# A gated cross-attention block in FP32 on one core: outputs of the last four pairs summed two by two in one PSUM bank

## The chip, the cores and the metric

The kernel runs on one core of one Trainium2 chip. A core has five engines that run side by side, each with its own queue of instructions: PE (matrix multiply, TensorE), DVE (VectorE), ACT (ScalarE), POOL (GpSimd) and SP (SyncE, which here only issues DMAs). They wait for each other through semaphores. Matmuls read SBUF and write PSUM, which has eight banks of 128 x 512 FP32 values; DVE and ACT read PSUM[...].

The metric is the device time of one execution in microseconds (us). Lower is better. Times in the profile count from the start of its span.

## The reference

32 sequences of 64 tokens, width 512, 32 heads of 128. Attention over a context, then a gated feed-forward layer with LoRA:

```python
q = (layernorm(x) @ Wq); k = (ctx @ Wk); v = (ctx @ Wv)          # split into 32 heads
score = einsum("bqhd,bkhd->bhqk", q, k) / sqrt(128) + position_bias   # masked keys: -inf
probs = softmax(score)
x = x + tanh(g0) * (einsum("bhqk,bkhd->bqhd", probs, v) @ Wo)
x = x + tanh(g1) * (layernorm(x) @ weight.T + bias + LoRA(layernorm(x)))
```

## The kernel before

The 2048 tokens are worked in two halves (`p` = 0, 1) of 1024. In a half, 16 pairs of heads (`n` = 0 to 15) follow each other. The times of half one stand below without a mark; half two repeats the same program on the other tokens.

**Numbers in two parts.** A FP32 product is made of three matmuls in FP32R: each operand is split into a high part (a cast on ACT) and a low part (operand minus high part, a subtraction on POOL or DVE), and `mm3` (L92) adds high x high, high x low and low x high into one bank. Products of keys, queries and values are done by Strassen's scheme with seven block products p1, p6, p7, p5, p2, p4, p3 (`unit`, L348), each of six matmuls of 128 x 512; p4 and p3 of a unit are worked after the first product of the next unit (`carry`). The seven blocks of the activations, high and low, fill seven big tiles, one for each name.

**Stages of a half.** `stage_a` (L654) makes keys and values of all pairs and stores them in device memory. `attention` (L739) then goes pair by pair: `q_unit` makes the queries; `scores` multiplies them with the keys (L807), adds bias and mask, takes the row maximum on DVE (L811) and subtracts it on POOL (L812); `exped` takes the exponential on ACT (L821); `normed` sums rows on DVE (L831 to L833) and scales on POOL (L834); `turn` transposes 32 x 32 blocks on DVE (L845), and `copy` (L842) places 32 x 256 pieces in the block diagonal tile `pts`, on ACT, or straight from the scores by a DVE transpose. `pv` (L938) multiplies values and probabilities into four banks (L943) and evicts each as high part `ch` on ACT (L946) and low part `cl` on DVE (L947). `prep_o` (L960) splits the output weight of a pair (L89 on ACT, L90 on POOL) from a raw tile fetched earlier; `oproj` (L973) multiplies `ch` and `cl` of a pair with it, tile of 128 tokens by tile, six matmuls each (`pa`), and adds the bank to the running output `acc` on DVE (L981).

**Order.** The program is written in order by hand; there is no scheduler. What goes beside the products is kept in generators in the list `streams`: each call of `beat()` after a product advances every stream by one step, and `drain` runs a stream to its end. So the order in the queue of each engine is fixed by where a stream starts and how many beats pass.

**The end of a half.** After the scores of pairs 14 and 15 the loop (L1076) does: output product 12 for tiles 0 to 5, first half of values 13, tiles 6 and 7 of product 12, second half of values 13, and the same for 13 with 14 and 14 with 15; then product 15. Weight 13 begins to be split (`start_o`) after tiles 0 to 5 of product 12, weights 14 and 15 one product later each. `last_turned` (L893) is the stream that normalizes and turns pairs 14 and 15; its inner `rest` turns pair 15. In half one, `next_blocks` (L455) splits the context of half two into its seven blocks beside this, on POOL mostly (raw `c1`, blocks `c1p`), and all are done before `stage_a` of half two starts. In half two, `ffn_weights` (L1128) splits the weights of the feed-forward layer instead, and `beside` works its first chunk (`ffn_tile`: transposes `tpf`; `ffn_lora`: products `pt`) between the tiles of output product 14.

Of the kernel before, what the change touches and what calls it, by code (L numbers as in the profile page):

```python
# [43 lines left out]
def flamingo_block(ctx: ExitStack, tc: tile.TileContext, x, xT, ctxT, bias, mask, gx, gf,  # L44
# [410 lines left out]
    def next_blocks(f, tags, nm, out):  # L455
        b11, b21, b12, b22 = parts(f)

        def block(q, raw, eng=nc.gpsimd):
            t = big(tags[ORDER.index(q)], [P, 2, 2, 512], F32R, f"{nm}{q}")
            out[q] = []  # L460
            for kt in range(2):
                split(raw[kt], t[:, 0, kt], t[:, 1, kt], eng)
                out[q].append((t[:, 0, kt], t[:, 1, kt]))
                yield

        def sub(o, a, b, eng=nc.gpsimd):
            for kt in range(2):
                eng.tensor_tensor(o[kt], a[kt], b[kt], ALU.subtract)
                yield

        yield from block("p1", b11)
        yield from block("p3", b22)
        yield from sub(b11, b12, b11)
        yield from sub(b12, b22, b12)
        yield from sub(b22, b22, b11, nc.vector)
        yield from block("p6", b22)
        yield from block("p7", b12)
        yield from block("p5", b11)
        yield from block("p2", b21)
        yield from sub(b21, b21, b22, nc.vector)  # L480
        yield from block("p4", b21, nc.vector)
# [172 lines left out]
    def stage_a(p, first, fc, res, rot, more, enter):  # L654
        xc, plain = first
        f = None
        for n in range(NPR):
            g = p * NPR + n
            if n == 0 and plain:
                sums = sum_blocks(fc, res, f"c{p}", nc.vector, xc)  # L660
                streams.append(sums)
            if n == (1 if plain else 0):
                streams.append(key_blocks(p, n + 1))
# [75 lines left out]
    def attention(p, res, rest, freed):  # L739
# [6 lines left out]
        def load_v(n, t=None, cs=None):  # L746
            b["v", n] = t or big(res[3], [P, NT, 256], F32, f"v{p}_{n}")
            for sl in [slice(c * 4, c * 4 + 4) for c in cs] if cs else [slice(0, NT)]:
                nc.sync.dma_start(out=b["v", n][:, sl], in_=vd[p][n // 2][:, sl, n % 2 * 256:(n % 2 + 1) * 256])
# [50 lines left out]
        acc, pts = [], []  # L800

        def scores(n, i, qT, kT):
            ps = psum(f"ps{p}_{n}_{i}", (P, NT, S))
            for t in range(NT):
                for h in range(2):
                    tok = slice(t * P + h * S, t * P + (h + 1) * S)
                    nc.tensor.matmul(ps[h * S:(h + 1) * S, t, :], qT[:, i, tok], kT[:, i, tok], start=True, stop=True)  # L807
            s = sm[n % 2][:, i]
            nc.vector.scalar_tensor_tensor(s, ps, SCALE, s, ALU.mult, ALU.add)
            mx = st.tile([P, NT], F32, tag="mx", name=f"mx{p}_{n}_{i}")  # L810
            nc.vector.tensor_reduce(mx, s, AX.X, ALU.max)  # L811
            nc.gpsimd.tensor_tensor(s, s, mx.unsqueeze(2).to_broadcast([P, NT, S]), ALU.subtract)  # L812
            beat()
            if n:
                streams.append(exped(s))
            else:
                nc.scalar.activation(s, s, AF.Exp)
# [75 lines left out]
        def last_turned():  # L893
            n = NPR - 2
            pts.append(big(res[1], [P, 2, NT, P], F32, f"pz{p}"))
            tp, todo = {}, []
            norm = both(normed(n, 0), normed(n + 1, 0))

            def turn_next(m, i):
                if i == 0:  # L900
                    tp[m] = [rows.tile([P, NT, S], F32, tag="row", name=f"tp{p}_{m}_{k}") for k in range(2)]
                turn(tp[m][i], m, i)
                todo.extend((m, i, q) for q in quads)
# [4 lines left out]
            def copies(k):  # L908
                for m, i, q in todo[:k]:
                    copy(nc.scalar.copy, m, i, tp[m][i], *q)  # L910
                del todo[:k]

            for k in range(14):
                if k in (0, 1, 8, 10):
                    next(norm)
                if k in (3, 5):
                    turn_next(n, k // 5)
                if k in (4, 9):
                    zero(k // 9)
                copies(2 if k in (4, 5, 8, 9, 12, 13) else 1)  # L920
                yield
            copies(16)

            def rest():
                for i in range(2):
                    turn_next(n + 1, i)
                    yield
                while todo:
                    copies(2)
                    yield  # L930
            b["s", n + 1] = rest()
            streams.append(b["s", n + 1])

        def both(*gs):
            for g in gs:
                yield from g

        def pv(n, cs=(0, 1)):  # L938
            drain(b["s", n])
            for i, c in [(i, c) for i in range(2) for c in cs] if n == 0 else [(i, c) for c in cs for i in range(2)]:  # L940
# [5 lines left out]
                nc.scalar.copy(ch[:, i, sl], ps)  # L946
                nc.vector.tensor_tensor(cl[:, i, sl], ps, ch[:, i, sl].bitcast(F32), ALU.subtract)  # L947
                beat()
            if NPR - 3 <= n < NPR - 1:
                load_v(n + 1, b["v", n], cs)  # L950
            elif n + 1 < NPR:
# [8 lines left out]
        def prep_o(n):  # L960
            raw = raw_of.pop(("o", p * NPR + n))
            t = big(res[2 if n in (NPR - 3, NPR - 1) else 4], [P, 2, 1024], F32R, f"wo{p}_{n}")
# [10 lines left out]
        def oproj(n, ts=range(NT), beside=None):  # L973
            drain(ob.get(n))
            w = b["o", n]
            for t in ts:
                ps = psum(f"pa{p}_{n}_{t}")
                sl = slice(t * P, (t + 1) * P)
                mm3(ps, [((ch[:, i, sl], cl[:, i, sl]),
                          (w[:, 0, i * 512:(i + 1) * 512], w[:, 1, i * 512:(i + 1) * 512])) for i in range(2)])  # L980
                nc.vector.tensor_tensor(acc[t], ps, acc[t], ALU.add)  # L981
                if n == NPR - 1 and p < NPH - 1:
                    nc.sync.dma_start(out=x1d[t * P:(t + 1) * P, :], in_=acc[t])
                beat()
                if beside:
                    beside(t)
# [8 lines left out]
        def run(xq, prefetch, before_last, last_unit, last, beside=None):  # L995
# [28 lines left out]
            def score(*ns):  # L1024
# [11 lines left out]
                elif n == NPR - 2:  # L1036
                    b["s", n] = last_turned()
# [23 lines left out]
            for a in range(4, NPR, 2):  # L1061
# [5 lines left out]
                if a < NPR - 2:  # L1067
                    oproj(a - 2)
                    start_o(a - 1)
# [5 lines left out]
            for n in range(NPR - 3, NPR):  # L1075
                oproj(n - 1, range(6), beside if n == NPR - 1 else None)  # L1076
                if n == NPR - 3:
                    start_o(n)
                pv(n, (0,))
                oproj(n - 1, range(6, NT))  # L1080
                pv(n, (1,))
                if n < NPR - 1:
                    start_o(n + 1)
            drain(ob[n])
            last(lambda t: oproj(n, range(t, t + 1)), acc)
# [42 lines left out]
    def ffn_weights(tags):  # L1128
# [6 lines left out]
        for _ in range(6):  # L1135
# [12 lines left out]
        for t in range(4):  # L1148
            ffn_norm(0, t)
            yield  # L1150
# [50 lines left out]
    def ffn_chunk(c, beside=lambda t: None):  # L1201
        more = c + 1 < NPH * NCH
        if c:
            ffn_lora(c)
# [10 lines left out]
    more = None  # L1215
    for p in range(NPH):
# [8 lines left out]
        enter, run = attention(p, res, rest, freed)  # L1225
        xq = stage_a(p, first, f, res, rot, more, enter)
        if p < NPH - 1:
# [10 lines left out]
            def last_unit():  # L1238
                blocks = paced(next_blocks(f, qt, f"c{p + 1}", first[0]), 2)
                keys = prep("k", g, nc.gpsimd, 36, then=lambda: fetch("k", g + 2, "r0"))  # L1240
                streams.extend((blocks, keys))
                parts_of.extend((blocks, keys))

            def last(o, acc):
                nonlocal more
                for t in range(NT):
                    o(t)
                for d in parts_of:
                    drain(d)
                more = acc_stats(p, acc)  # L1250
            parts_of = []
            run(xq, prefetch, before_last, last_unit, last)
        else:
# [4 lines left out]


            def beside(t):  # L1260
                if t == 0:
                    drain(weights)
                if t < 4:
                    ffn_tile(0, t)
                elif t == 4:
                    ffn_lora(0)
                else:
                    ffn_norm(1, 0)

            def last(o, acc):  # L1270
                acc1.extend(acc)

                def moments(t):
                    ln_moments(acc[t], mv2[:, p * NT + t, :], f"r{p}_{t}")

                def rstd_of(c):
                    for _ in ln_rstd(mv2[:, c * 4:(c + 1) * 4, :], f"f{c}", rstd, c, 5, nc.gpsimd):
                        pass

                def rest_of(t):  # L1280
                    if t < 2:
                        moments(4 + 2 * t)
                        moments(5 + 2 * t)
                    if t == 1:
                        rstd_of(NPH * NCH - 1)
                    if t == 3:
                        ffn_norm(2, 0)

                for t in range(NT):
                    o(t)  # L1290
                    if t < 4:
                        moments(t)
                    if t == 3:
                        rstd_of(NPH * NCH - 2)
                ffn_chunk(0, rest_of)
                ffn_chunk(1, lambda t: ffn_norm(3, 0) if t == 3 else None)
                ffn_chunk(2)
                ffn_chunk(3)
            run(xq, ffn_fetch, ffn_rows, last_unit, last, beside)
# [45 lines left out]
```

## Time and profile before

| what | us |
|---|---|
| median of three runs | 1537.7 (1535.86 to 1538.94) |
| profiled execution | 1537.11 |
| its span, first to last instruction | 1535.3 |
| PE busy | 1522.2 (99%) |
| POOL busy | 1045.5 (68%) |
| DVE busy | 959.8 (63%) |
| ACT busy | 727.5 (47%) |
| mean DMA rate | 162 GB/s |

A line of groups in the profile gives: source line, engine, operation, output and input tiles, sizes and count, then busy time and mean nanoseconds of one, then the idle time of the engine just before them and what ended it. A line of waits gives: who waited for whom, total us, how often, longest. A line of the timeline gives: start, length, engine, line, operation, tiles, count, and in brackets the idle time before it and its releaser. The time of a matmul in a row is longer than its step, since matmuls overlap. A busy PE is no PE at full speed: at half clock it is busy too.

### The profile page before, as it was taken

How to read it: one execution, taken by the hardware profiler on the slowest of the kernel's cores; microseconds unless marked ns; L12 is line 12 of the kernel's file. 1: busy time of each engine (PE TensorE's matmuls, PEld its weight loads, DVE VectorE, ACT ScalarE, POOL GpSimd, SP SyncE). 2: the span in 40 equal slices, each digit the busy share in tenths (PEclk: the TensorE clock that was granted, in tenths of full speed). 3: DMA queues.
4: the chain of work that ended last, by engine and by line, in shares of the span. 5: the costliest groups of instructions: out<-in, count | busy, mean ns of one | idle time of the engine just before them, and what ended most of it. 6: DMA issues, size and time to landing. Idle time of an engine off the chain costs nothing.

```text
span 1535.3 us, 25153 instructions
## 1 busy us (share of the span) xinstructions
PE 1522.2 (99%) x8988; PEld 1282.3 (84%) x8988; DVE 959.8 (63%) x1599; ACT 727.5 (47%) x1602; POOL 1045.5 (68%) x1154
## 2 busy tenths in 40 slices
PE   9999999999999999999999999999999999999998
PEld 7888888888888888887888888888888888888787
DVE  5665554376676567667476558437657666766764
ACT  6444233355654565467344423335566456546611
POOL 3898478968665667577789847896866666656210
PEclk9999999999999999999999999999999999999999
DMA  6754544384244354522575454438425435442311
GB/s 216 264 192 151 199 165 167 138 309 172 102 150 167 107 210 138 179 83 83 200 253 202 154 201 168 168 140 315 158 89 170 147 132 185 151 166 78 96 42 69
DMA packets 111135, 248.51 MB, mean 162 GB/s; under 512 B 10305, under 2 KB 44097, under 8 KB 106914
## 3 DMA queue, kind: packets, MB, share of 16 engines
q1 hardware_dynamic: 110722, 246.38, 45.7%
q8 instruction: 71, 1.16, 0.3%
q10 hardware_dynamic: 288, 0.52, 0.1%
q14 instruction: 54, 0.44, 0.1%
HBM read 173.45 MB, written 73.42 MB: 161 GB/s over the span
## 4 chain that ended last, share of the span: by engine, by line
PE 96%; DVE 1%; POOL 1%; ACT 1%; issue 0%; DMA 0%; DVEq 0%; POOLq 0%; ACTq 0%
PE pa L98 23%; PE po L943 7%; PE pzv L98 6%; PE pvv L98 6%; PE pxv L98 6%; PE pxq L98 5%; PE pzq L98 5%; PE pvq L98 5%; PE pzk L98 5%; PE pvk L98 5%; PE pxk L98 5%; PE ps L807 4%; PE pyv L98 3%; PE pf L98 3%; PE pyq L98 3%; PE pyk L98 3%
## 5 line engine op out<-in xcount | busy, mean ns | idle before, releaser
L98 PE MATMUL pa<-wo,ch 128*128 128x512 f32 x1024 | 321.9, 395 | 6.3 <-POOL wo L90 3.4
L98 PEld LDWEIGHTS pa<-wo,ch 128*128 128x128 f32 x1024 | 191.1, 189 | 47.8 <-POOL wo L90 5.2
L842 ACT COPY pt<-tp 32x256 f32<-32x256 f32 x472 | 190.4, 403 | 68.1 <-DVE tp L845 57.1
L981 DVE TENSOR_TENSOR acc<-pa,acc 128x512 f32<-128x512 f32 x256 | 171.2, 679 | 57.0 <-PE pa L98 56.9
L98 PE MATMUL pa<-wo,cl 128*128 128x512 f32 x512 | 200.7, 392 | 0.0
L760 POOL TENSOR_TENSOR sm<-sm,madd 128x512 f32<-128x512 f32 x60 | 76.8, 1293 | 107.2 <-DMA sm<-bias 107.2
L947 DVE TENSOR_TENSOR cl<-po,ch 128x512 fp32r<-128x512 f32 x128 | 87.7, 691 | 58.7 <-ACT ch L946 58.2
L834 POOL TENSOR_TENSOR sm<-sm,r 128x512 f32<-128x512 f32 x64 | 67.0, 1046 | 76.6 <-DVE r L833 69.0
L943 PEld LDWEIGHTS po<-pt,v 128*128 128x128 f32 x960 | 112.5, 192 | 3.6 <-ACT pt L842 0.9
L98 PEld LDWEIGHTS pa<-wo,cl 128*128 128x128 f32 x512 | 96.7, 189 | 20.8 <-DVE cl L947 0.5
L943 PE MATMUL po<-pt,v 128*128 128x128 f32 x960 | 113.1, 275 | 0.6 <-DVE pt L842 0.6
L356 DVE TENSOR_TENSOR vt<-pvv,vt 128x512 f32<-128x512 f32 x64 | 44.1, 689 | 93.3 <-PE pvv L98 93.3
L90 POOL TENSOR_TENSOR wo<-rawo,wo 128x512 fp32r<-128x512 f32 x64 | 82.3, 1309 | 28.3 <-ACT wo L89 17.5
L946 ACT CAST ch<-po 128x512 fp32r<-128x512 f32 x128 | 75.0, 589 | 46.4 <-PE po L943 44.4
L812 POOL TENSOR_TENSOR sm<-sm,mx 128x512 f32<-128x512 f32 x64 | 67.0, 1051 | 43.0 <-DVE mx L811 43.0
L356 DVE TENSOR_TENSOR qT<-pvq,qT 128x512 f32<-128x512 f32 x64 | 44.1, 690 | 73.1 <-PE pvq L98 73.0
L356 DVE TENSOR_TENSOR kT<-pvk,kT 128x512 f32<-128x512 f32 x60 | 41.3, 688 | 76.2 <-PE pvk L98 76.2
L378 ACT COPY vt<-pxv 128x512 f32<-128x512 f32 x32 | 18.9, 589 | 130.9 <-PE pxv L98 130.9
L821 ACT ACTIVATE sm<-sm 128x512 f32<-128x512 f32 x60 | 38.0, 633 | 85.6 <-POOL sm L812 82.4
L356 DVE TENSOR_TENSOR qT<-pzq,qT 128x512 f32<-128x512 f32 x64 | 44.2, 691 | 37.8 <-PE pzq L98 37.6
L807 PEld LDWEIGHTS ps<-kB,qT 128*64 128x64 f32 x2048 | 61.3, 138 | 4.2 <-issue 2.1
L192 POOL TENSOR_TENSOR vs<-wvr,wvr 128x512 f32<-128x512 f32 x24 | 31.3, 1313 | 49.2 <-DMA wvr<-wv 49.2
(992 smaller groups left out, 3777.2 us busy)
## 6 DMA issues: line engine op xcount, KB each, us to landing
kd<-kT SPq DMA_DIRECT2D x64, 512.0 KB, 3.8
vd<-vt SPq DMA_DIRECT2D x128, 256.0 KB, 2.4
kB<-kd SPq DMA_DIRECT2D x32, 1024.0 KB, 10.0
v<-vd SPq DMA_DIRECT2D x28, 1024.0 KB, 7.9
rawq<-wq SPq DMA_DIRECT2D x32, 512.0 KB, 3.3
sm<-bias SPq DMA_DIRECT2D x64, 256.0 KB, 5.0
rawo<-wo SPq DMA_DIRECT2D x32, 512.0 KB, 3.6
rawk<-wk SPq DMA_DIRECT2D x31, 512.0 KB, 5.3
```

The source lines that it names most:

```text
L90: eng.tensor_tensor(lo, raw, hi.bitcast(F32), ALU.subtract)
L98: nc.tensor.matmul(ps, a, b, start=start and i == 0, stop=stop and i == 3 * n - 1, skip_group_check=True)
L356: nc.vector.tensor_tensor(o, ps, i, ALU.add)
L760: nc.gpsimd.tensor_tensor(t, t, masks[p][0], ALU.add)
L807: nc.tensor.matmul(ps[h * S:(h + 1) * S, t, :], qT[:, i, tok], kT[:, i, tok], start=True, stop=True)
L812: nc.gpsimd.tensor_tensor(s, s, mx.unsqueeze(2).to_broadcast([P, NT, S]), ALU.subtract)
L834: nc.gpsimd.tensor_tensor(t, t, r.unsqueeze(2).to_broadcast([P, NT, S]), ALU.mult)
L842: f(pts[n == NPR - 2][dst, i, :, src], of[src, :, ki * 32:(ki + 1) * 32])
L943: nc.tensor.matmul(ps[:, t * P:(t + 1) * P], b["v", n][:, c * 4 + t, i * P:(i + 1) * P], pts[n == NPR - 2][:, i, c * 4 + t, :], start=True ...
L946: nc.scalar.copy(ch[:, i, sl], ps)
L947: nc.vector.tensor_tensor(cl[:, i, sl], ps, ch[:, i, sl].bitcast(F32), ALU.subtract)
L981: nc.vector.tensor_tensor(acc[t], ps, acc[t], ALU.add)
```

## The change

The end of each half is worked in another order.

- Pairs 12 and 13, and 14 and 15, share their output products: `oproj2` adds both pairs' matmuls (12 for each tile) in one bank, and DVE adds it to `acc` once.
- All values of 13 are multiplied right after the last scores, before any output product of 12. Values 14 and 15 are multiplied half by half between the two joint products' parts: first halves after tiles 0 to 5 of 12+13, second halves after tiles 6 and 7.
- `ch` and `cl` of pairs 13 and 15 lie in two other big tiles (`more_ctx`, the places of activation blocks p2 and p4); weight 13 lies in p5's place, weights 14 and 15 in the two tiles of the queries.
- Weight 13 begins to be split before the last scores, weight 14 after values 13, weight 15 after the first part of the joint product.
- `last_turned` turns both pairs in 16 steps; pair 15's second head goes by direct DVE transposes.
- Three of the seven context blocks of half two wait for these tiles: p5 until all values are read, p2 and p4 until the half has ended. p2 and p4 are then split on DVE within the first key unit of half two.
- The row maxima have four small buffers instead of two.
- In half two the norms, moments and transposes of chunk 0 go beside the last joint product, and its LoRA product stands in `ffn_chunk` behind them.

```diff
-    def next_blocks(f, tags, nm, out):
+    def next_blocks(f, tags, nm, out, gate):
...
         yield from block("p7", b12)
+        while not gate:
+            yield
         yield from block("p5", b11)
-        yield from block("p2", b21)
+        while len(gate) < 2:
+            yield
+        yield from block("p2", b21, nc.vector)
         yield from sub(b21, b21, b22, nc.vector)
         yield from block("p4", b21, nc.vector)
...
+            if n == 1 and not plain:
+                drain(blocks)
...
-            mx = st.tile([P, NT], F32, tag="mx", name=f"mx{p}_{n}_{i}")
+            mx = st.tile([P, NT], F32, tag="mx", name=f"mx{p}_{n}_{i}", bufs=4)
...
+            direct = [(n + 1, 1, q) for q in quads]
...
+            for k in range(16):
+                if k in (1, 3, 6, 8):
                     next(norm)
+                if k in (4, 5):
+                    turn_next(n, k - 4)
+                if k in (5, 7):
+                    zero(k // 7)
+                if k == 9:
+                    turn_next(n + 1, 0)
+                if k > 5:
+                    for of, m, i, q in todo[:3]:
+                        copy(nc.scalar.copy, m, i, of, *q)
+                    del todo[:3]
+                if k > 10:
+                    for m, i, q in direct[:2]:
+                        copy(nc.vector.transpose, m, i, sm[m % 2][:, i], *q)
+                    del direct[:2]
+                yield
...
-            t = big(res[2 if n in (NPR - 3, NPR - 1) else 4], [P, 2, 1024], F32R, f"wo{p}_{n}")
+            if n < NPR - 2:
+                t = big(qt[3] if n == NPR - 3 else res[4], [P, 2, 1024], F32R, f"wo{p}_{n}")
+            else:
+                t = kqp.tile([P, 2, 1024], F32R, tag="kq", name=f"wo{p}_{n}")
...
+        def oproj2(n, ts, lead, beside=None):
+            drain(ob[n])
+            ts = list(ts)
+            for group in [ts[:lead]] + [[t] for t in ts[lead:]]:
+                ps = [psum(f"pa{p}_{n}_{t}") for t in group]
+                for k, t in enumerate(group):
+                    mm3(ps[k], o_terms(n, t), stop=False)
+                    beat()
+                drain(ob[n + 1])
+                for k, t in enumerate(group):
+                    mm3(ps[k], o_terms(n + 1, t), start=False)
+                    nc.vector.tensor_tensor(acc[t], ps[k], acc[t], ALU.add)
...
+                    beat()
+                    if beside:
+                        beside(t)
...
-                    start_o(a - 1)
+                start_o(a - 1)
+                if a < NPR - 2:
                     pv(a - 1)
                 score(a, a + 1)
...
-            for n in range(NPR - 3, NPR):
-                oproj(n - 1, range(6), beside if n == NPR - 1 else None)
-                if n == NPR - 3:
-                    start_o(n)
-                pv(n, (0,))
-                oproj(n - 1, range(6, NT))
-                pv(n, (1,))
-                if n < NPR - 1:
-                    start_o(n + 1)
-            drain(ob[n])
-            last(lambda t: oproj(n, range(t, t + 1)), acc)
+            n = NPR - 4
+            load_v(n + 3)
+            pv(n + 1)
+            start_o(n + 2)
+            oproj2(n, range(6), 3)
+            start_o(n + 3)
+            for c in range(2):
+                if c:
+                    oproj2(n, range(6, NT), 1)
+                pv(n + 2, (c,))
+                pv(n + 3, (c,))
+            values_read(acc)
+            oproj2(n + 2, range(NT), 2, beside)
...
-        for _ in range(6):
+        for _ in range(8):
             yield
...
-        if c:
-            ffn_lora(c)
+        ffn_lora(c)
...
             def beside(t):
-                if t == 0:
-                    drain(weights)
                 if t < 4:
-                    ffn_tile(0, t)
-                elif t == 4:
-                    ffn_lora(0)
+                    ffn_norm(0, t)
+                    moments(t)
                 else:
-                    ffn_norm(1, 0)
+                    ffn_tile(0, t - 4)
+                if t == 4:
+                    rstd_of(NPH * NCH - 2)
```

## The prediction

> **What bounds the kernel now.** I read the page first. Its line of PE says 99% busy and its chain of waits puts 96% on PE, so only time in which PE stands or runs slowly can be won or lost. The waits of PE say where it stands:
>
> ```profile
> PE   9999999999999999999999999999999999999998
> PE pa L98 <- POOL wo L90: 3.4, 4, 1.0
> PE pa L98 <- ACT wo L89: 2.8, 2, 1.7
> ```
>
> Both are output products (pa) waiting for a split output weight. The timeline puts them at the end of each half, where pair 13's weight comes too late:
>
> ```profile
> 693.09 0.62 ACT L89 CAST wo<-rawo 128x512 fp32r<-128x512 f32 x1
> 693.76 0.50 PE L98 MATMUL pa<-wo,ch 128*128 128x512 f32 x1 [1.67 <-ACT wo L89]
> 695.12 0.50 PE L98 MATMUL pa<-wo,ch 128*128 128x512 f32 x1 [0.85 <-POOL wo L90]
> ```
>
> The windows of that stage give the length, then busy PE, and third from the end the granted clock:
>
> ```profile
> 1418.60:1421.50 2.90, 0.73 (x4) 0.22 (x2) 1.39 (x3) 2.82 (x7) 2.53 (x3) 0.94 0.00 0
> 1421.50:1428.00 6.50, 5.47 (x12) 3.92 (x13) 6.15 (x11) 5.01 (x12) 3.66 (x3) 0.50 0.41 127
> 690.00:697.00 7.00, 3.91 (x23) 2.83 (x22) 5.90 (x11) 6.79 (x16) 5.84 (x6) 1.00 0.08 28
> ```
>
> A matmul of 512 columns starts every 0.227 us (six take 1.36 in the timeline). Gaps over that step in the PE rows are 3.7 us at 691.8 to 696.5, and 6.4 us at 1418.5 to 1428, of which 3.0 us are some fifteen matmuls at half clock: 10.1 us in all. Check: 192 output matmuls (43.6) and three value products (3.5 each) make 54.1 us of work after half one's last score; PE took from 677.33 to 735.74, 58.4.
>
> What the new order asks for hangs on the softmax of pairs 14 and 15, which starts here in the two halves:
>
> ```profile
> 676.72 2.54 POOL L760 TENSOR_TENSOR sm<-sm,madd 128x512 f32<-128x512 f32 x2 [10.58 <-DMA sm<-bias]
> 1403.56 2.54 POOL L760 TENSOR_TENSOR sm<-sm,madd 128x512 f32<-128x512 f32 x2 [9.38 <-DMA sm<-bias]
> ```
>
> POOL had idled 10 us for pair 15's bias. The durations I use:
>
> ```profile
> L812 POOL TENSOR_TENSOR sm<-sm,mx 128x512 f32<-128x512 f32 x64 | 67.0, 1051 | 43.0 <-DVE mx L811 43.0
> L834 POOL TENSOR_TENSOR sm<-sm,r 128x512 f32<-128x512 f32 x64 | 67.0, 1046 | 76.6 <-DVE r L833 69.0 <-ACT pt L842 5.5 <-DMA sm<-bias 1.2
> L90 POOL TENSOR_TENSOR wo<-rawo,wo 128x512 fp32r<-128x512 f32 x64 | 82.3, 1309 | 28.3 <-ACT wo L89 17.5 <-PE tpf L137 10.8
> L947 DVE TENSOR_TENSOR cl<-po,ch 128x512 fp32r<-128x512 f32 x128 | 87.7, 691 | 58.7 <-ACT ch L946 58.2
> L468 DVE TENSOR_TENSOR c<-c,c 128x512 f32<-128x512 f32 x4 | 5.4, 1352 | 0.8 <-POOL c1p L90 0.8
> L842 DVE STREAM_TRANSPOSE pt<-sm 32x256 f32<-32x256 f32 x8 | 3.4, 423 | 0.1
> ACT sm L821 <- POOL sm L812: 82.4, 59, 5.6
> ```
>
> [...]
>
> **The change part by part.**
> *Nothing on PE goes.* The matmuls of the tail are the same. 32 of the 64 adds into acc in the two tails go, 32 x 0.68 = 22 us of DVE, beside matmuls: worth 0.
>
> *Weight 13 early* (start_o before the last scores): the 10.1 us go, half clock included. But its two POOL subtractions (2 x 1.31) now stand among the maxima subtractions of pairs 14 and 15.
>
> *Values 13 ahead of the output products, all evicted before product 12+13.* Half one, POOL without a break from 676.72 in the new order: mask twice 2.54, L812 of 14, context block p1 1.31, weight 13 1.31, L812, weight 13, L812 of 15: 2.54 + 3 x 1.05 + 3 x 1.31 = 9.6, to 686.3. ACT has exp of 15 first half (0.63), then the first eviction of values 13 (0.59): 687.6. Next in ACT is block p3's cast and the second exp of 15, for which POOL does p1's other half and L812 (2.4, to 688.7); exp to 689.35, the second eviction to 689.95, its low part on DVE (0.69) to 690.65. PE: values 13 from 677.33 to 680.8, 18 matmuls of pair 12 (4.1) to 684.9. The first tile's six matmuls of pair 13 would end at 686.3; their last needs the low part of 690.65 and ends at 690.9. **Lost 4.6.** The evictions stand behind the exponentials[...].
>
> *Values 14 and 15 both before tiles 6 and 7 of product 12+13.* Before, 15's came 25 us later. POOL goes on after DVE's row sum of 14 (1.1, to 691.75): two L834 of 14, p3 1.31, two context differences 1.27, weight 14 2 x 1.31, L834 of 15, a difference 1.29, L834 of 15: 12.0 with 0.2 of waiting, to 703.9. DVE then makes 15's second head by eight direct transposes (8 x 0.42), with two L468 (2.7) and an add (0.68) between: 6.8, to 710.7. PE: 690.9 + 2 x 1.36 + 3 x 2.72 = 701.8, values 14 first half 1.75, values 15 would end at 705.3. It ends at 711.6. **Lost 6.3.** The copies of 15's first head on ACT (tp at 702.8, 8 x 0.40) end at 706, inside this.
>
> *Half two*, with no context blocks but the FFN weights: POOL 1403.56 + 2.54 + 3 x 1.05 + 2 x 1.31 = 1411.9; exp and eviction 1413.1, second exp and eviction 1414.35, low part 1415.05; PE stands ready at 1411.7 and ends the tile at 1415.3 instead of 1413.05: **lost 2.2.** Then the row sums (14's second L834 ends 1419.7), b2 1.28, weight 14, a2 0.60, weight 14, wf 1.28, L834, wf twice, L834: 10.4, to 1430.15; DVE eight transposes and an add 4.1, to 1434.2; values 15 end at 1435.1 instead of 1429.7: **lost 5.4.**
>
> *Three context blocks late.* p5 fits on POOL under the last products. p2 (two casts and two DVE subtractions) starts when acc's last add is done, 0.9 us after the last product, and has the 5.4 us of p1, p6, p7, p5 in key unit 16: its second low part is due at about the last use, 0. p4 needs two L468-like differences (0.7 each, POOL then on weights) and two casts behind them; its product in unit 17 follows 2.7 us after p2's start: **lost 0.7**, bounds 0 and 3 (if DVE's differences take 1.35 each and wait for the p2 adds).
>
> *LoRA of chunk 0* moves directly behind the last transposes. In the timeline before, those started at 1446.53, ACT's cast ended at 1447.75, DVE's low part at 1448.48, and a product of 1.36 us lay between. Now nothing does: **lost 1.5.** Moments and norms go beside the joint products (2.3 us of DVE in 2.72): 0. mx with four buffers frees DVE's 4.1 us of waits for L812, none of it PE's: 0. SP: weight 14's fetch waits for weight 13's subtraction, and values 15 and 14 stand behind it (685 in half one); 8 us (the longest landing of v) brings them before 696, needed at 701: 0.
>
> Sum: 4.6 + 6.3 + 2.2 + 5.4 + 0.7 + 1.5 = 20.7 against 10.1 removed: +10.6. The profiled execution took 1537.1 (span 1535.3 and 1.8 around it), 0.6 under the median of 1537.7. So 1547.7. Clock: after half one's first gap, its second (3.7 us at a stretch) and half two's second (twice 2.4) the half clock can come, at 3.0 us each by the one case seen; bounds 0 and 9. I take one: **1550.5.**
>
> **Rivals.**
> *More clock:* all three gaps lower it, 1547.7 + 9 = 1556.7. For: each is longer than the gap that did it before. Against: half one's did not.
> *Chain shorter than my sum:* if POOL's neighbours run at the low end and DVE's differences at 0.7, second gaps shrink to about 4 and 4 and no clock falls: 1537.1 + 4.6 + 4 + 2.2 + 4 + 0.7 + 1.5 - 10.1 = 1544; with first gaps halved too, 1540.5.
> *The faster side:* both softmax chains end before PE asks. Then what is removed stays removed: 1537.1 - 10.1 + 2.2 (p4, LoRA) = 1529. Its place is the bias of pair 15: it decides where the mask starts some 6 us before 676.72 in half one, since POOL's chain then ends before each of PE's two dates. For: the DMA share is 0.00 in the windows after 677, so the bias is not far from being early. Against: no load ahead of it in SP's queue is moved.
> *The sums are not what was late:* joint tiles save only DVE adds, and the gaps move without changing, 1537.
>
> **Numbers.** Forecast 0.55, more clock 0.20, shorter chain 0.13 (most at 1541 to 1546), gaps equal 0.05, faster 0.07. From no change this kernel can be told by about 0.2%, 3 us. Faster 0.07, same 0.07 (gaps equal and the edge of the shorter chain), slower 0.86. The forecast's own bounds are 1543 to 1557; down to 1537 and up to 1561 no more than 2 in 10 is left out.
>
> **What would show it.** Waits of PE on values' evictions (po's ch and cl) and on the DVE transposes, and no more on weights; about 4.6 and 6 us idle at 685 to 711, 2 and 5 at 1412 to 1435; half clock behind one of them; key unit 16 starting near 743 without the clock. It is wrong if PE runs through 685 to 711, or if the span is under 1541.

## The result, and the profile after

The changed kernel takes 1548.99 us in the median of 6 runs (1547.82 to 1551.27); the kernel before, run beside it, 1537.74 (1535.86 to 1538.94). The ratio is 1.0075 with an interval of 1.0062 to 1.0088: slower by 11.3 us. The profiled execution has a span of 1547.7 us, 12.4 more than before.

The page of the changed kernel first: its head, its line of busy times and PE's row of the 40 slices.

```profile
span 1547.7 us, 25053 instructions
...
PE 1529.2 (99%) x8988; PEld 1285.1 (83%) x8988; DVE 948.0 (61%) x1583; ACT 719.2 (46%) x1586; POOL 1041.8 (67%) x1152
...
PE   9999999999999999999999999999999999999899
```

PE is still 99% busy, so the 12 us must again be short stretches in which PE stands or runs slowly. The waits of PE in the changed kernel (engine, line, what it waited for: us in total, times, longest) name them:

```profile
PE po L949 <- ACT pt L847: 4.4, 2, 2.3
PE po L949 <- DVE pt L847: 4.1, 4, 1.9
PE pa L98 <- ACT cx L953: 2.3, 2, 1.3
...
PE pt L1197 <- ACT fa L1189: 0.7, 1, 0.7
PE pvk L98 <- ACT c1p L89: 0.6, 1, 0.6
PE pvk L98 <- DVE c1p L90: 0.4, 2, 0.2
```

The two waits on a split weight (wo), which bound the kernel before, are gone. In their place stand the transposed probabilities of pair 15 (pt), the evicted values of pair 13 (cx), the transposes of chunk 0 ahead of the LoRA product (fa) and the late context blocks (c1p). The windows of these places in the changed kernel (window and length; busy time of PE, of its weight loads, of DVE, ACT and POOL, each with the number of instructions; then the granted clock, the DMA share and GB/s):

```profile
684.00:692.00 8.00, 5.74 (x18) 3.77 (x17) 3.54 (x8) 5.37 (x11) 6.26 (x7) 0.80 0.67 217
702.00:713.00 11.00, 7.20 (x40) 6.34 (x39) 10.05 (x19) 8.57 (x18) 7.39 (x7) 0.84 0.04 8
1420.00:1423.00 3.00, 3.00 (x11) 1.53 (x10) 1.98 (x3) 3.00 (x7) 0.51 (x1) 1.00 0.94 314
1434.00:1448.00 14.00, 9.80 (x46) 8.20 (x45) 8.97 (x18) 7.26 (x16) 6.59 (x6) 0.76 0.24 78
```

A busy share can hide a slow engine (from 688.78 to 692.19 PE is busy for 3.09 of 3.41 us at a granted clock of 0.50), so I also took every PE matmul's start to the next one's start from the trace and subtracted the normal step of its size (0.227 us at 512 columns, 0.112 at 128). What is left is split into standing and half clock (a step of 0.427 in place of 0.227, or 0.213 in place of 0.112); where the two meet in one step, the split is good to about 0.2. In us:

| place | predicted | standing | half clock |
|---|---|---|---|
| half one, values 13 (685 to 692) | 4.6 | 3.3 | 1.2 |
| half one, values 15 (703 to 713) | 6.3 | 4.7 | 1.3 |
| half two, values 13 (1420 to 1423) | 2.2 | 0.8 | 0 |
| half two, values 15 (1434 to 1447) | 5.4 | 5.3 | 2.2 |
| block p4 in key unit 17 (750 to 754) | 0.7 | 1.8 | 0 |
| LoRA of chunk 0 (1477 to 1479) | 1.5 | 1.4 | 0 |
| half clock, all | 3.0 | | 4.7 |
| sum | 23.7 | 17.3 + 4.7 = 22.0 | |

The same reckoning of the kernel before gives 3.9 us at 691 to 697 and 4.9 + 1.6 at 1418 to 1428: 10.4 removed. 22.0 - 10.4 = 11.6 of the 12.4 us by which the span grew; the rest is spread over smaller steps. The gaps do account for the result.

The first place in half one, from the timeline of the changed kernel (start, length, engine, line; in brackets the idle time before it and who ended it):

```profile
676.44 2.52 POOL L765 TENSOR_TENSOR sm<-sm,madd 128x512 f32<-128x512 f32 x2 [10.08 <-DMA sm<-bias]
...
685.73 0.63 ACT L826 ACTIVATE sm<-sm 128x512 f32<-128x512 f32 x1 [1.62 <-POOL sm L817]
686.26 0.57 ACT L953 CAST cx<-po 128x512 fp32r<-128x512 f32 x1
...
686.86 0.69 DVE L954 TENSOR_TENSOR cx<-po,cx 128x512 fp32r<-128x512 f32 x1 [6.37 <-ACT cx L953]
...
687.95 0.63 ACT L826 ACTIVATE sm<-sm 128x512 f32<-128x512 f32 x1 [0.60 <-POOL sm L817]
688.48 1.05 ACT L953 CAST cx<-po 128x512 fp32r<-128x512 f32 x2
```

Each eviction (L953) runs directly behind an exponential (L826) that waited for POOL, as the prediction had it. The bracket of the DVE line shows something more: DVE too stood 6.37 us behind the first eviction, and pair 14's row sums queue behind that. This turned out to matter.

### The profile page after: what moved, and what is told of

Read it like the earlier page. It is cut to its first block, busy times and chain, and to the rows that moved or that the text cites. A ratio compares the mean times of both kernels' runs of the same rounds, so it can differ in the third digit from the quotient of the medians.

```text
span 1547.7 us, 25053 instructions
## 1 busy us (share of the span) xinstructions
PE 1529.2 (99%) x8988; PEld 1285.1 (83%) x8988; DVE 948.0 (61%) x1583; ACT 719.2 (46%) x1586; POOL 1041.8 (67%) x1152
## 4 chain that ended last, share of the span: by engine, by line
PE 91%; DVE 3%; POOL 2%; issue 1%; DMA 1%; ACT 1%; SPq 0%; DVEq 0%; POOLq 0%; ACTq 0%
PE pa L98 21%; PE po L949 7%; PE pzv L98 6%; PE pvv L98 6%; PE pxv L98 6%; PE pzk L98 5%; PE pvk L98 5%; PE pxq L98 5%; PE pxk L98 5%; PE pzq L98 5%; PE pvq L98 5%; PE ps L812 3%; PE pyv L98 3%; PE pyq L98 3%; PE pyk L98 3%; PE pf L98 2%
## 5 line engine op out<-in xcount | busy, mean ns | idle before, releaser
L98 PE MATMUL pa<-wo,ch 128*128 128x512 f32 x896 | 280.3, 394 | 0.0
L847 ACT COPY pt<-tp 32x256 f32<-32x256 f32 x456 | 183.9, 403 | 64.0 <-DVE tp L850 53.0
L98 PEld LDWEIGHTS pa<-wo,ch 128*128 128x128 f32 x896 | 167.5, 189 | 34.8
L98 PE MATMUL pa<-wo,cl 128*128 128x512 f32 x448 | 175.5, 392 | 0.0
L993 DVE TENSOR_TENSOR acc<-pa,acc 128x512 f32<-128x512 f32 x192 | 129.3, 681 | 53.5 <-PE pa L98 53.5
L954 DVE TENSOR_TENSOR cl<-po,ch 128x512 fp32r<-128x512 f32 x112 | 76.4, 691 | 47.4 <-ACT ch L953 47.0
L98 PEld LDWEIGHTS pa<-wo,cl 128*128 128x128 f32 x448 | 84.5, 189 | 18.5 <-DVE cl L954 0.6
L953 ACT CAST ch<-po 128x512 fp32r<-128x512 f32 x112 | 65.6, 590 | 59.7 <-PE po L949 58.0
L826 ACT ACTIVATE sm<-sm 128x512 f32<-128x512 f32 x60 | 38.0, 633 | 83.9 <-POOL sm L817 80.7
L812 PE MATMUL ps<-kB,qT 128*64 128x64 f32 x2048 | 64.1, 223 | 0.3 <-DVE qT L356 0.3
```

Source lines behind the costliest of these rows:

```text
L98: nc.tensor.matmul(ps, a, b, start=start and i == 0, stop=stop and i == 3 * n - 1, skip_group_check=True)
L847: f(pts[n == NPR - 2][dst, i, :, src], of[src, :, ki * 32:(ki + 1) * 32])
L953: nc.scalar.copy(h[:, i, sl], ps)
L954: nc.vector.tensor_tensor(lo[:, i, sl], ps, h[:, i, sl].bitcast(F32), ALU.subtract)
```

## Experiments

Ten kernels, all of them edits of the changed kernel. Each ratio is to the kernel before, run beside it; differences from the changed kernel (1.0075) are taken from these ratios, times 1538. The intervals of two ratios leave such a difference uncertain by some 2 to 3 us; what is said of single places comes from the traces, one execution each.

### Pair 15's exponentials behind the evictions

```
-                streams.append(exped(s))
+                streams.append(exped(s, 4 if n == NPR - 1 else 0))
...
-        def exped(s):
+        def exped(s, wait):
+            for _ in range(wait):
+                yield
             nc.scalar.activation(s, s, AF.Exp)
```

> Pair 15's two exponentials are issued four steps later, so that the four evictions of values 13 stand ahead of them on ACT; nothing else moves. Both theories expect the first place of half one (3.0 us standing and some 1.35 of half clock at 685 to 692) to come down to under 0.7. Theory one date: the heads of values 15 come from a chain over POOL, ACT and DVE that doesn't wait for PE, so PE reaches it earlier and stands there longer by what it saved: the second place of half one grows from 4.2 to about 8 us, and the time is 1548 to 1549, within 1.5 of the changed kernel. Theory added gaps: each gap is its own loss, the second stays at 4.2, and the time falls by about 4.4, to 1544.5. Half two changes by less than 1 in either.

Measured: 1544.32 us, ratio 1.0044 (1.0030 to 1.0059), 4.8 us below the changed kernel. The first place of half one is gone in full (3.3 and 1.2 to 0), so the evictions were late because of the exponentials ahead of them on ACT. The second place there grew, from 4.7 to 6.4, which is 1.7 for the 4.5 that PE came earlier. Neither theory is right. The added gaps hit the time (1544.5), but by luck: 1.7 us came back in half one, and half two gave some 3 us in place of under 1. The two places hang together in part. Two lines of ACT and DVE in this kernel's timeline show how:

```profile
683.95 0.57 ACT L953 CAST cx<-po 128x512 fp32r<-128x512 f32 x1
684.55 0.69 DVE L954 TENSOR_TENSOR cx<-po,cx 128x512 fp32r<-128x512 f32 x1 [3.75 <-ACT cx L953]
```

DVE now stands 3.75 us and not 6.37, the row sum of pair 14 behind it starts at 686.17 and not at 689.69, and the whole chain to values 15 ends some 1.9 us earlier (the last direct transpose at 707.2 against 709.1). One late eviction had held PE directly and the softmax of pair 14 by way of DVE. Half two moved in the same way, by more than the 1 us expected: DVE stood 2.88 us there behind the first eviction and not 5.13, the second place fell from 5.3 to 3.9 us standing, the first from 0.8 to 0.

### Values 15 behind tiles 6 and 7

```
-            for c in range(2):
-                if c:
-                    oproj2(n, range(6, NT), 1)
-                pv(n + 2, (c,))
-                pv(n + 3, (c,))
+            pv(n + 2, (0,))
+            oproj2(n, range(6, NT), 1)
+            pv(n + 3, (0,))
+            pv(n + 2, (1,))
+            pv(n + 3, (1,))
```

> The first half of values 15 is taken behind tiles 6 and 7 of product 12+13 (5.4 us of matmuls) and behind nothing else. Theory one date: the second places (4.2 us standing in half one, 4.95 in half two, and some 1.55 and 2.6 of half clock behind them) go, 13.3 us in all; weight 15's split then ends at the old date (POOL to 711.75 and 1442 in the changed kernel) and PE can ask for it some 2 us earlier in each half, so 1535.7 without that wait and 1539.7 with it. Rival, the chain moves with PE: the two adds of the joint tiles that now come ahead of the transposes on DVE wait for PE and hold the transposes back, so the places shrink by less than half: 1543 or more.

Measured: 1535.23 us, ratio 0.9985 (0.9979 to 0.9992): 13.8 us below the changed kernel, and faster than the kernel before. The windows of half one:

```profile
684.00:692.00 8.00, 5.88 (x18) 3.65 (x17) 3.79 (x8) 5.26 (x10) 6.26 (x7) 0.86 0.81 258
702.00:713.00 11.00, 11.00 (x74) 9.97 (x73) 10.78 (x20) 9.08 (x19) 7.37 (x7) 1.00 0.03 7
```

PE fills the second window without a break and at full clock, while the first place stands as before (8.00 with 5.88 busy). With the half clock behind them, the second places cost 13.5 us in the changed kernel, and what is left of them is 0.1 and 0.5. The wait for weight 15 did not come. That values 15 were asked for 5.4 us of matmuls too early in each half is thus worth more than the whole loss.

### The context blocks of half two begun later

```
+        for _ in range(7):
+            yield
         yield from block("p1", b11)
```

The stream is paced by two, so this holds it back 14 steps.

> The context blocks of half two begin 14 steps later in half one, so that none of their subtractions on POOL stands ahead of pair 15's softmax; half two is not touched. Theory POOL: seven POOL instructions of 1.3 us leave the chain; the second eviction of values 13 comes 2.2 us earlier and the first place falls from 3.0 us to about 0.6, its half clock with it; the chain to values 15 ends 6 us earlier on POOL but then hangs on ACT's copies, so the second place falls from 4.2 to about 2: some 6 us less, 1543 (1541 to 1546). Half two's places stay (0.8 and 4.95). Rival, ACT's and DVE's queues set the dates: under 1 us. Up to 3 us can come back where the blocks now end later, in the first key units of half two.

Measured: 1543.94 us, ratio 1.0034 (1.0021 to 1.0047), 6.3 us below the changed kernel. By places, in half one: the first 3.3 to 0.7 standing, the second 4.7 to 3.1; half two's second 5.3 to 4.9. POOL's share of the chain is shown. That the second place stops at 3.1 was not tested; the waits put it down to ACT's copies, on which PE now stands there for 2.8 us at a stretch:

```profile
PE po L951 <- ACT pt L849: 5.1, 2, 2.8
PE po L951 <- DVE pt L849: 1.8, 3, 1.2
```

(Lines are two further down in this kernel.) Nothing came back in the first key units: the product with p4 lost 1.8 as in the changed kernel.

### Two sums in place of the joint one

```
-                    mm3(ps[k], o_terms(n, t), stop=False)
+                    mm3(ps[k], o_terms(n, t))
+                    nc.vector.tensor_tensor(acc[t], ps[k], acc[t], ALU.add)
+                    ps[k] = psum(f"pb{p}_{n}_{t}")
...
-                    mm3(ps[k], o_terms(n + 1, t), start=False)
+                    mm3(ps[k], o_terms(n + 1, t))
```

> Each joint output tile is made as two sums again, with two adds into acc instead of one; order, buffers and all else stay as in the changed kernel. That puts back 32 DVE adds of 0.68 us. Theory adds cost nothing: 1549 within 1. Rival, DVE's queue is on the path to values 15: four to six adds more stand ahead of the direct transposes in each half, the second places grow by 1.4 to 2 each, 1552 to 1553.

Measured: 1555.85 us, ratio 1.0112 (1.0097 to 1.0127), 5.7 us above the changed kernel. The rival holds, and at more than its size: the second places stand 9.7 and 7.8 us (4.7 and 5.3 in the changed kernel). The waits of PE:

```profile
PE po L949 <- DVE pt L847: 6.3, 4, 4.1
PE po L949 <- ACT pt L847: 5.6, 2, 2.8
PE po L949 <- DVE acc L1010: 2.2, 2, 1.7
```

The wait for the direct transposes grew by 2.2 us, and a new one appeared: a bank of the values waits for an add. In the new order the adds are not beside the path; they stand in the DVE queue that it runs through. The edit also takes a second bank for each tile, so the 5.7 us are the price of the adds and of their banks together.

### The direct transposes in one step

```
-                    for m, i, q in direct[:2]:
+                    for m, i, q in direct[:8]:
...
-                    del direct[:2]
+                    del direct[:8]
```

> The eight direct transposes of pair 15's second head are issued in one step, where the changed kernel issues two in each of four steps with adds into acc (0.69 each) and, in half one, two context differences (0.69 each) between them. No work is added or taken out. Theory DVE queue: in half one they start at the old date (703.3) and take 8 x 0.44 = 3.5 us, so they end at 706.9 instead of 709.1, and the second place there falls from 4.7 us standing by 2.2, to about 2.5; its first half, which waits for ACT's copies, stays. In half two they wait for POOL until 1436.9 and end 0.7 earlier, and the second place falls from 5.3 to 4.6. 2.9 us less in all, 1546, or a little less still if half clock goes with it. Rival, ACT's copies or POOL's products with the row sums end last: under 0.7 us, 1548 to 1549.

Measured: 1544.29 us, ratio 1.0045 (1.0029 to 1.0062), 4.6 us below the changed kernel. In the changed kernel DVE stood like this at the second place of half one:

```profile
703.34 0.86 DVE L847 STREAM_TRANSPOSE pt<-sm 32x256 f32<-32x256 f32 x2
704.21 0.69 DVE L468 TENSOR_TENSOR c<-c,c 128x512 f32<-128x512 f32 x1
704.93 0.88 DVE L847 STREAM_TRANSPOSE pt<-sm 32x256 f32<-32x256 f32 x2
705.83 0.69 DVE L1008 TENSOR_TENSOR acc<-pa,acc 128x512 f32<-128x512 f32 x1
706.53 0.89 DVE L847 STREAM_TRANSPOSE pt<-sm 32x256 f32<-32x256 f32 x2
707.45 0.69 DVE L468 TENSOR_TENSOR c<-c,c 128x512 f32<-128x512 f32 x1
708.18 0.89 DVE L847 STREAM_TRANSPOSE pt<-sm 32x256 f32<-32x256 f32 x2
```

and with the transposes in one step:

```profile
702.78 3.56 DVE L847 STREAM_TRANSPOSE pt<-sm 32x256 f32<-32x256 f32 x8
...
1432.62 3.58 DVE L847 STREAM_TRANSPOSE pt<-sm 32x256 f32<-32x256 f32 x8 [1.61 <-POOL sm L839]
```

The same eight transposes end at 706.3 and not at 709.1: 2.2 us of it since the three instructions that had stood between the pairs now come after them, and 0.6 since DVE reached them earlier in this execution. The second places fall to 1.9 and 3.9 us standing, and the 1.3 of half clock in half one goes with them. In half two 0.7 was expected and 1.4 measured: the transposes end 0.7 earlier there against POOL's last product, as expected, and what the rest hangs on was not shown. No work was added or removed, so the place of these instructions in DVE's queue is what was worth it; this is the same cause as in the run with two sums, seen from the other side.

### Block p4 and the LoRA product

```
         yield from block("p5", b11)
+        yield from sub(b11, b21, b22)
...
-        yield from sub(b21, b21, b22, nc.vector)
-        yield from block("p4", b21, nc.vector)
+        yield from block("p4", b11, nc.vector)
...
-                else:
-                    ffn_tile(0, t - 4)
+                if 3 <= t < 7:
+                    ffn_tile(0, t - 3)
```

> Two small edits of the changed kernel in two places far apart. The difference of block p4 is made early on POOL, into the buffer that p5 has read, so that only casts and low parts stand behind p2; the transposes of chunk 0 begin one output tile earlier, so that a product of 2.7 us lies between the last of them and the LoRA product. Theory: the 1.8 us at the product with p4 in key unit 17 fall to under 0.4, the 1.4 us ahead of the LoRA product to under 0.2, about 2.8 in all, 1546.2. Rival: the queues of DVE and ACT that make p2 hold p4 as well, and the earlier transposes wait for the norms on DVE: under 1 us in all.

Measured: 1547.17 us, ratio 1.0066 (1.0053 to 1.0080), not told apart from the changed kernel by the times. By places, the LoRA product's 1.4 fell to 0.2, so the missing cover was its cause. The product with p4 only fell from 1.8 to 1.6:

```profile
748.42 0.62 ACT L89 CAST c1p<-c 128x512 fp32r<-128x512 f32 x1
...
749.15 2.26 DVE L90 TENSOR_TENSOR c1p<-c,c1p 128x512 fp32r<-128x512 f32 x2 [1.52 <-ACT c1p L89]
```

The differences are off the path, but p4's first cast still starts only at 748.42, 4.0 us after p2's second cast had ended, and the two low parts take 2.26 on DVE, beside POOL's weight work. What holds the cast back, the pacing of the stream or a queue, is told apart further below.

### The order of before

```
-            pv(n + 1)
-            start_o(n + 2)
-            oproj2(n, range(6), 3)
...
+            for m in (n + 1, n + 2):
+                oproj(m - 1, range(6))
+                pv(m)
+                oproj(m - 1, range(6, NT))
+                start_o(m + 1)
+            pv(n + 3)
```

> The changed kernel with the order of before for pairs 12 to 14: two sums for 12 and 13, each one's values behind six tiles of the product ahead; pairs 14 and 15 stay joint, their values 15 last. Weight 13's early start, the buffers, the context blocks and the LoRA product stay as changed. It puts 16 DVE adds back. Theory: without the new order both new waits at values 13 and 15 go and what the early weight 13 removed stays removed: 1537.7 - 10.1 + 1.8 + 1.4 = 1530.8. Rival, the early weight brings nothing by itself and the place moves to the next wait: 1537 or more.

Measured: 1535.32 us, ratio 0.9986 (0.9980 to 0.9993), 2.2 us faster than before where 6.9 were expected. No wait for a weight is left, so the early weight 13 does remove what it was credited with. The two new places are gone as well. But the place of half one took a new wait, on the low parts of values 13 and on an add:

```profile
PE pa L98 <- DVE cx L954: 1.8, 2, 1.1
PE pa L98 <- DVE acc L993: 1.4, 1, 1.4
```

That is 2.4 and 1.8 us standing at 684 to 713; with p4's 1.8 and LoRA's 1.4 kept from the change, the gain of the early weight is largely given back. The theory falls in its size.

### Together

The exponentials, values 15 behind tiles 6 and 7, p4 and LoRA in one kernel:

> Three edits together: pair 15's exponentials behind the evictions of values 13, the first half of values 15 behind tiles 6 and 7, and the two small edits. From the kernel with values 15 late (1535.2): its first places (2.6 and 0.5 us standing and 1.3 of half clock) go, 4.4; where the exponentials alone were moved the chain to values 15 came 2.6 us earlier for 4.35 that PE came earlier, so up to 1.7 us of the second place of half one come back; p4 and LoRA bring 2.8. 1529.7, and 1528 to 1532. Rival, what is freed at one date is waited for at the next (weight 15, the copies on ACT): above 1533.

Measured: 1529.95 us, ratio 0.9955 (0.9941 to 0.9968). Both places of values 13 are gone; 0.8 us of the second place of half one came back. Then the context blocks begun later on top (five steps of the paced stream in place of seven, and the early difference without steps of its own):

> As the kernel with three edits, and the context blocks of half two begun 10 steps later in half one, so that one pair of their POOL subtractions and no more stands ahead of pair 15's softmax. Theory POOL: the second place of half one (up to 1.7 us) goes, and 1528 is reached, 0 to 1.7 below the kernel with three edits. Rival: weight 15's split, which now stands behind four more POOL instructions of 1.3 us, and the blocks in the first key unit of half two come late: 1 to 4 us above it.

Measured: 1528.70 us, ratio 0.9947 (0.9934 to 0.9959). The 0.8 us fell to 0.1, as the theory of POOL had it, though the two kernels' intervals overlap; weight 15 did not come late. The windows of the places of half one, all of PE busy at full clock:

```profile
684.00:692.00 8.00, 8.00 (x37) 6.64 (x36) 7.03 (x15) 6.92 (x16) 6.44 (x7) 1.00 0.89 293
702.00:713.00 11.00, 11.00 (x75) 10.01 (x74) 8.82 (x14) 7.04 (x14) 8.10 (x7) 1.00 0.16 49
```

The one place left was the product with p4, 1.6 us. So in the last kernel p2 and p4 are issued in one step:

```
-        yield from block("p2", b21, nc.vector)
-        yield from block("p4", b11, nc.vector)
+        for _ in both_of(block("p2", b21, nc.vector), block("p4", b11, nc.vector)):
+            pass
+        yield
```

> The kernel with four edits, and in it blocks p2 and p4 issued in one step of the stream, so that p4's two casts stand directly behind p2's on ACT and its low parts behind p2's on DVE, ahead of the evictions of key unit 16. Theory pacing: p4's first cast had ended up to 4 us after p2's second only because a paced stream issued it later; now it comes directly behind, and the 1.6 us at the product with p4 fall to under 0.3, 1527.4. Rival, ACT's and DVE's queues: the four low parts on DVE (0.69 to 1.2 each) push the evictions of key unit 16 back and PE waits for them or for p2's low parts instead: the same 1.6 us or more, 1528.7 to 1530.

Measured: 1527.17 us (1526.94 to 1527.51), ratio 0.9927 (0.9914 to 0.9941). The timeline of this kernel shows the four casts and the four low parts in one piece, and the evictions of key unit 16 behind them:

```profile
734.45 2.18 ACT L89 CAST c1p<-c 128x512 fp32r<-128x512 f32 x4
735.10 2.50 DVE L90 TENSOR_TENSOR c1p<-c,c1p 128x512 fp32r<-128x512 f32 x4 [1.86 <-ACT c1p L89]
737.52 0.68 DVE L356 TENSOR_TENSOR kT<-pyk,kT 128x512 f32<-128x512 f32 x1
```

The place is gone (1.6 to 0), and PE waits for none of the evictions: the pacing was the cause. The intervals of this kernel and of the one without this edit overlap, so it is the trace that shows it. The earlier issue also kept most of the low parts clear of POOL: the four took 2.50 us together, POOL's weight work for the next unit began only at 737.0, and two alone had taken 2.26 beside it.

This kernel is 0.7% faster than the one before and 1.5% faster than the changed one. The parts of the change are all in it; only the order of their pieces in the queues is different.

## Why the prediction was right, point by point

It said slower, 1550.5 us; it was 1548.99, with the waits where it had put them. The sum came nearer than its terms, and that part is luck: the six places cost 17.3 us standing where it had 20.7, the half clock 4.7 where it had 3.0, and 10.4 went where it had 10.1. (1547.7 and 3.0 make 1550.7; the 1550.5 is a slip of 0.2.)

*Weight 13 early, 10.1 us removed:* right (10.4 by the finer reckoning); no wait for a weight is left.

*Values 13, half one, 4.6:* the cause is right and shown by moving the exponentials. 3.3 us stood: POOL began 0.3 earlier (676.44) and the scores ended 0.35 later (677.68) than the sum had it, so PE came later and found the chain further on.

*Values 15, half one, 6.3:* right place, 4.7 us. The mis-sized term is the two differences L468, taken at 1.35 each, the mean of four that had taken 0.68 to 1.80. They took 0.69 each. POOL stood idle beside the first of them; in the kernel before, one had taken 1.80 at 701.26 with POOL on weight subtractions. Beside the second it was POOL's subtraction that took longer, 1.69 at 707.59 in place of 1.3. Beside POOL's weight work at 749 two of the same DVE differences took 0.68 and 1.22. What makes these times differ was not tested. ACT's copies, which the sum had as hidden and done at 706, were done at 706.3: PE stood first behind them, for 2.3 us, and then behind the transposes.

*Values 13, half two, 2.2:* the term that was most wrong in proportion. 0.8 us: PE came at 1420.57 and the first eviction began at 1420.08. The sum had used the distance from POOL's start to the end of the scores in the kernel before; that distance grew from 0.5 us (1403.56 to 1404.07) to 1.27 (1411.51 to 1412.78).

*Values 15, half two, 5.4:* 5.3. *LoRA, 1.5:* 1.4, and gone once a product covers it.

*p4, 0.7:* 1.8, inside its bounds of 0 to 3. The differences and low parts on DVE took 0.91 and 0.92 in the mean, beside POOL, and not 0.7, and the sum had left out that a paced stream issues p4's casts some steps after p2's; issued in one step with p2, the wait is gone.

*One loss of clock at 3.0:* it came three times and cost 1.2, 1.3 and 2.2. The count was wrong, and the size of one too: by the finer reckoning the case it was taken from had cost 1.6, and the rest of the 3.0 was standing. The sum, 4.7, was nearer the one taken than either bound, which is luck: that the half clock would come once was an estimate, and which gaps bring it is not shown (last section).

*32 DVE adds worth 0:* wrong where it matters. In the kernel before no wait of PE names them; in the new order DVE's queue sets the date of values 15, and with two sums for each tile, and a second bank for them, the changed kernel lost a further 5.7 us. The prediction priced the adds by what lay beside them before, not by the queue that the change itself made critical.

*The rival on the faster side* hung on the bias of pair 15 landing earlier: POOL still idled 10.08 us for it in half one and 8.91 in half two. Its reason for, no DMA after 677, holds in the kernel before only to 685.4; from there to 700 the share was 0.25. What the rival described, both chains done before PE asks, is what the reordered kernels reached by the other way, PE asking later.

The places were summed as if each loss stood for itself. The moved exponentials show that this held only in part: of 4.5 us saved at the first place, 1.7 came back at the second.

## What to carry to other kernels

Ask of a moved product not only whether its inputs are computed in time, but which queue their last instruction stands in: here exponentials ahead of evictions on ACT, and adds and differences between transposes on DVE, cost more than the work itself, and reordering them without removing any gained 4.6 to 4.8 us each. When work is fused to save instructions on an idle engine, price it again in the new order, where that engine may be the bound. Before taking a new order back, put the covering matmuls between the late input and its use: one reordering of four calls turned 0.75% slower into 0.15% faster. And count short gaps together: those at 685 to 689 in the changed kernel, none of them over 1.5 us, were followed by 3.41 us at half clock, which cost another 1.2 us.

## What the runs showed of the hardware

The traces hold the moments at which the granted clock changed. Up to the last 5 us of each execution it was half from 1421.16 to 1427.99 in the kernel before (6.83 us), and from 688.78 to 692.19, from 709.26 to 712.67 and from 1439.71 to 1446.54 in the changed kernel (3.41, 3.41 and 6.83 us). Here it did not follow the length of a gap. First three stretches of the kernel before, whose 3.9 us standing in half one brought no half clock, then three of the changed kernel, whose 3.3 us were followed by it:

```profile
690.71:694.12 3.41, 1.74 (x14) 1.37 (x12) 2.65 (x4) 3.30 (x8) 2.51 (x3) 1.00 0.00 1
694.12:697.53 3.41, 1.99 (x8) 1.22 (x8) 2.98 (x7) 3.29 (x9) 3.14 (x3) 1.00 0.02 5
697.53:700.95 3.42, 3.42 (x17) 2.82 (x16) 3.32 (x7) 3.09 (x7) 3.30 (x4) 1.00 0.82 280
...
685.37:688.78 3.41, 1.47 (x5) 0.48 (x3) 0.69 (x1) 2.46 (x5) 3.41 (x4) 1.00 0.69 215
688.78:692.19 3.41, 3.09 (x7) 2.44 (x8) 3.04 (x7) 2.80 (x6) 1.67 (x3) 0.50 0.95 314
692.19:695.60 3.41, 3.41 (x16) 2.81 (x15) 2.65 (x6) 1.70 (x5) 3.31 (x4) 1.00 0.69 238
```

In the kernel before PE was busy for 3.73 of the 6.82 us of the first two stretches, with one gap of 1.67 us in that place, and the clock stayed at 1.00. In the changed kernel it was busy for 1.47 of the 3.41 us from 685.37, with no single gap over 1.5 us, and the next 3.41 us ran at 0.50. These are single executions: they do not show which gaps bring half clock. Its price is the slower matmuls in it, a step of 0.427 us in place of 0.227: 1.2 to 2.2 us for each of the three times in the changed kernel. Of the kernel before, 66 executions with their mean granted clock are on record: the two at 0.995 took 1539.64 and 1541.01 us, the two at 1.000 took 1535.01 and 1535.44.

The order of the instructions on ACT and DVE reached further than one wait: in the changed kernel a single eviction held DVE for 6.37 us and moved the softmax of another pair by 3.5 (its row sum at 689.69, against 686.17 with the exponentials moved).
